# The first pass of a macaron block: when projection weights, tokens and normalisation scales are loaded

## Chip, cores and metric

One core of a Trainium2 chip runs the whole program in one launch. The metric is the device time in microseconds (us), as the median of several runs; a profile of one more execution says where the time goes. The core's engines are TensorE (PE, matrix products into PSUM), VectorE (DVE), ScalarE (ACT, activations with a scale and a bias), GpSimd (POOL) and SyncE (SP, which here only issues transfers). Each engine executes its own instructions in the order in which the program lists them, and semaphores order the engines among each other.

## The reference

The input is 4 x 1024 tokens of 1024 float32 values. Every block works on normalised tokens and adds its result to the tokens:

```python
x = x + 0.5 * ffn(layernorm(x), weight, bias, centroids, assignments)
x = x + attn(layernorm(x), Wq, bq, Wk, bk, Wv, bv)
x = x + 0.5 * ffn(layernorm(x), weight, bias, centroids, assignments)

def ffn(x, ...):                       # 1024 -> 1024, gated
    dots = softmax(x @ centroids.T / 0.1, axis=-1)     # 64 clusters
    hits = dots > 0.01
    query_sel, cluster_sel = any(hits, axis=1), any(hits, axis=0)
    row_sel = cluster_sel[assignments]
    dense = x @ weight.T + bias
    return where(query_sel[:, None] & row_sel[None, :], dense, 0)

def attn(x, ...):                      # per token, over the 32 x 32 head dimension
    q, k, v = projections of x with 32, 8 and 8 heads; k, v repeated 4 times
    scores = einsum('bsdh,bseh->bsde', q, k) / sqrt(32)
    return einsum('bsde,bseh->bsdh', softmax(scores), v)
```

Because `cluster_sel` is taken over all tokens, no row of the first FFN can be masked before the logits of all tokens are known. This divides the kernel into three passes over the tokens.

## The kernel before

The 4096 tokens are `NT` = 32 tiles of 128 tokens. In the first pass the FFN product of every tile is made and stored (`d1`); the second adds it masked, makes the attention and the logits of the second FFN; the third makes the second FFN's product and the output. The change lies in the first pass alone.

The first pass has steps t = 0 to 31. Two tiles a, a+1 are multiplied together in `winograd`: seven block products of four 128-deep blocks each (tile `st`, L284), in place of eight. A pair takes two steps: the odd step t (a = t - 3) issues four of the products, the next even step the other three. Additions of the products into the result `d` (L275) are DVE's work, straight out of PSUM, and some products accumulate onto a bank that an addition has read before. The last 256 columns and the 64 logits of a tile are made apart: in steps up to 7 and from 28 on by `logits` (tile `ff`, L212), one per step; for the tiles 8 to 27 (`GATED`) by `last_two` (tile `la`, L348), which runs beside `winograd` in the same steps. Steps 8, 9 and 10 hold neither: they have only the three, four and three products of the pairs (4, 5) and (6, 7).

PE needs a tile transposed (`xT`). Tiles 0 to 4 are normalised and transposed on PE. From tile 5 (`BLOCKED`) on it goes another way, over several steps:

- `load_x` (L152) loads the tile token by row, as `x`, only for its moments: `moments` takes two `bn_stats` (L162) on DVE and a root on ACT (L165), `scales` a reciprocal (L171) and a product (L173) on DVE. `block_scales` stores the two numbers of each token in DRAM as `scd`, with a transfer issued by ACT (L648).
- `spread` (L497) loads them as `scb`, so that each partition has the scales of four tokens; it takes four transfers, one for each strip of 32 partitions.
- `load_blocks` (L490) loads the tile a second time as `xb`, in blocks of 32 tokens by 32 columns, with four transfers.
- `from_blocks` normalises the four parts of `xb` on ACT (L505, four activations) and transposes the blocks on DVE (L509).
- `token_sums` makes the four sums that `winograd` needs of a pair, on POOL (L257 to L260), in the odd steps.

What is done in which step is written out by hand. Step t first issues on SP the loads of x(t+5) and xb(t+4) (`loads`), then `spread(t+3)`, and in odd steps two stores of `d1`. `block_scales(t+4)`, the step's logits, the first product with its addition, and `from_blocks(t+1)` follow. At the end of the step the generator `weights` issues a transfer of the projections' weights, which the second pass needs, and one step later does the work on it: `wq` (tile `qn`, L582, 512 KB) in steps 3 to 10 with a reduction on DVE (L586, 1.21 us), `wk` and `wv` (tile `kv`, L597, 128 KB each) in steps 11 to 18 with two copies on POOL (L602), then four blocks of the FFN's weights from SBUF to DRAM (`wtd`, L628). `x`, `xb`, `xT`, `d`, `qn`, `kv` and the token sums all take their place from one pool of `ROWS` = 26 rows of 4 KB per partition; a new row may wait for the last user of the old one.

Of the kernel before, what the change touches and what calls it, by code (L numbers as in the profile page):

```python
# [15 lines left out]
P = 128  # L16
# [26 lines left out]
def kernel(  # L43
# [97 lines left out]
    def strip(i):  # L141
        return slice(i * QROW, (i + 1) * QROW)

    def rows(ap, t):
        return ap[t * P : (t + 1) * P, :]

    def row(name):
        return data.tile([P, EMB], F32, tag="row", bufs=ROWS, name=name)
# [321 lines left out]
    with (  # L470
# [21 lines left out]
        def spread(flat, t):  # L492

            sb = small.tile([P, 4, 2], F32, tag="scb", bufs=4, name=f"scb{t}")
            src = flat.rearrange("(i t) e -> t i e", i=4)
            for j in range(4):
                nc.sync.dma_start(out=sb[strip(j)], in_=src)  # L497
            return sb

        def from_blocks(t, sb):  # L500

            b = xb.pop(t)
            for i in range(4):
                bi = b[:, :, i]
                nc.scalar.activation(  # L505
                    bi, bi, AF.Identity, bias=sb[:, i, 1:2], scale=sb[:, i, 0:1]
                )
            t_ = row(f"xT_1_{t}")
            nc.vector.transpose(t_, b.rearrange("p k i c -> p (k i c)"))  # L509
            return t_.rearrange("p (k c) -> p k c", c=P)  # L510
# [61 lines left out]
        columns(6)  # L572
        ahead(1)

        def weights(step):


            if step < KT:

                k = step  # L580
                qn = row(f"qn{k}").rearrange("p (c r) -> p c r", r=REP)
                nc.sync.dma_start(  # L582
                    out=qn, in_=wq[k * P : (k + 1) * P].rearrange("p d (g r) -> p (d g) r", r=REP)
# [5 lines left out]
                    AX.X,  # L589
                    ALU.add,  # L590
                )
            elif step < 2 * KT:
                k = step - KT
                kvs = row(f"kv{k}")
                kv = {i: kvs[:, (i - 1) * D * HKV : i * D * HKV] for i in (1, 2)}
                for i, src in ((1, wk), (2, wv)):
                    nc.sync.dma_start(  # L597
                        out=kv[i], in_=src[k * P : (k + 1) * P].rearrange("p d h -> p (d h)")
                    )
                yield  # L600
                for i in kv:
                    nc.gpsimd.tensor_copy(  # L602
                        by_head(wqkv[:, k, :], i), kv[i].rearrange("p (d h) -> p d h", h=HKV)
                    )
            elif step == NT - 6:
                bn = row("bn_q").rearrange("p (c r) -> p c r", r=REP)
                nc.sync.dma_start(
                    out=bn.rearrange("p c r -> p (c r)"),
                    in_=bq.rearrange("d h -> (d h)").partition_broadcast(P),
                )  # L610
                bss = row("bs")
                bs = {i: bss[:, (i - 1) * D * HKV : i * D * HKV] for i in (1, 2)}
                for i, src in ((1, bk), (2, bv)):
                    nc.sync.dma_start(
                        out=bs[i], in_=src.rearrange("d h -> (d h)").partition_broadcast(P)
                    )
                yield
                nc.vector.tensor_reduce(
                    by_head(bqkv, 0), bn.rearrange("p (d g) r -> p d g r", g=HKV), AX.X, ALU.add
                )  # L620
                for i in bs:
                    nc.gpsimd.tensor_copy(
                        by_head(bqkv, i), bs[i].rearrange("p (d h) -> p d h", h=HKV)
                    )
            elif step < 2 * KT + 5:

                i = step - 2 * KT - 1
                nc.sync.dma_start(out=wtd[i], in_=blocks(wc)[i])  # L628
            elif step == 2 * KT + 6:
                next(qsums)  # L630
            elif step == NT - 7:
                asg = load_assigned()
                yield
                hot.append(one_hot(asg))

        pending = iter(())
        sc, sb, ss, es, ge = {}, {}, {}, {}, {}
# [4 lines left out]
        qts = w12, w11, w21, w22  # L642
        qsums = weight_sums(blocks(wqkv), qts, [nc.gpsimd] * 4)

        def block_scales(t):
            sc[t] = dram.tile([P, 2], F32, tag="scd", bufs=5, name=f"scd{t}")
            own = scales(moments(xt.pop(t), f"1_{t}"), f"1_{t}")
            nc.scalar.dma_start(out=sc[t], in_=own)  # L648

        def loads(t):  # L650
            if t + 5 < NT:
                load_x(t + 5, rows(xf, t + 5), 1)
            if BLOCKED <= t + 4 < NT:
                load_blocks(t + 4)

        def logits(t):
            dt_[t] = row(f"d1_{t}")
# [3 lines left out]
        for t in range(3):  # L661
# [13 lines left out]
            if t + 2 < BLOCKED:  # L675
                ahead(t + 2)
            for i in (5, 6) if t == 2 else ():
                block_scales(i)

        for t in range(3, NT):  # L680

# [4 lines left out]
            if t % 2 == 1 and t > 4:  # L686
                for i in (a, a + 1):
                    nc.sync.dma_start(out=d1[i], in_=dt_.pop(i))
            if t + 4 < NT:
                block_scales(t + 4)  # L690
            if t not in GATED:
                es[t] = logits(t)
            if t == 3:
# [8 lines left out]
                    steps = zip(steps, last_two(a, a + 1, s4, te, ge))  # L702
            if t < NT - 1:
                next(steps)
            if t > 3:
                i = t + 1
                if i in sb:
                    xT[i] = from_blocks(i, sb.pop(i))
            for i in sorted(es):
                if i >= t - 3 and not isinstance(es[i], tuple):  # L710
                    es[i] = gate_exp(es[i], i, 0)
# [14 lines left out]
                ss[t - 1] = token_sums(xT, t - 1, t, 1)  # L726
            for _ in pending:
                pass
            pending = weights(t - 3)
            next(pending, None)  # L730


# [484 lines left out]
```

## Time and profile before

| | us |
|---|---|
| median of 3 runs | 1323.7 (1322.91 to 1324.2) |
| the profiled execution | 1323.88 |
| its span, first to last instruction | 1322.2 |
| TensorE busy in it | 1301.0 (98%) |
| VectorE, GpSimd, ScalarE busy | 871.0, 583.3, 495.1 |
| mean granted TensorE clock | 0.997 of full speed |

The page also says that the span moved 214.25 MB at a mean of 162 GB/s. In the lines further down, a row of a timeline gives start and duration in us, then engine, line, operation and the tiles written and read; in brackets stands the idle time before it and what ended that. In the chain of waits (the work that ended last, followed back from the end) a row gives start, duration and what it was. A row of the waits gives who waited for what, the total in us, the number of waits and the longest. "SPq" is SP's queue. Matmuls overlap a little, so that eight of 128x384 show 2.74 us in the timeline and 2.58 in the chain.

### The profile page before, as it was taken

How to read it: one execution, taken by the hardware profiler on the slowest of the kernel's cores; microseconds unless marked ns; L12 is line 12 of the kernel's file. 1: busy time of each engine (PE TensorE's matmuls, PEld its weight loads, DVE VectorE, ACT ScalarE, POOL GpSimd, SP SyncE). 2: the span in 40 equal slices, each digit the busy share in tenths (PEclk: the TensorE clock that was granted, in tenths of full speed). 3: DMA queues.
4: the chain of work that ended last, by engine and by line, in shares of the span. 5: the costliest groups of instructions: out<-in, count | busy, mean ns of one | idle time of the engine just before them, and what ended most of it. 6: DMA issues, size and time to landing. Idle time of an engine off the chain costs nothing.

```text
span 1322.2 us, 22786 instructions
## 1 busy us (share of the span) xinstructions
PE 1301.0 (98%) x8726; PEld 840.5 (64%) x8726; DVE 871.0 (66%) x1789; ACT 495.1 (37%) x821; POOL 583.3 (44%) x448
## 2 busy tenths in 40 slices
PE   8998999999999999999999999999999999999998
PEld 7664677777776665666666666666666655555554
DVE  4655555555546358888888888778867448555556
ACT  4432223333210445666666666666643200000000
POOL 3621132232112147566666666666532326634440
PEclk9999899999999999999999999999999999999999
DMA  8487876778614155456666665665551346655532
GB/s 297 86 161 146 170 146 139 167 180 173 124 64 191 43 166 160 153 191 189 195 200 195 189 198 166 200 200 189 163 156 26 104 139 227 239 200 176 178 114 80
DMA packets 296301, 214.25 MB, mean 162 GB/s; under 512 B 240064, under 2 KB 255168, under 8 KB 296192
## 3 DMA queue, kind: packets, MB, share of 16 engines
q1 hardware_dynamic: 278240, 164.78, 46.5%
q0 software_dynamic: 8736, 30.68, 6.3%
q10 hardware_dynamic: 9216, 17.33, 3.6%
q8 instruction: 69, 1.13, 0.4%
q14 instruction: 40, 0.33, 0.1%
HBM read 127.77 MB, written 84.96 MB: 161 GB/s over the span
## 4 chain that ended last, share of the span: by engine, by line
PE 93%; DMA 2%; DVE 2%; ACT 1%; issue 1%; POOL 0%; SPq 0%; ACTq 0%; POOLq 0%; DVEq 0%
PE st L284 40%; PE qs L801 18%; PE ff L212 16%; PE la L348 6%; PE tp L205 4%; PE pq L212 4%; PE sc L877 2%; PE po L919 2%; DMA x<-in_L_attn_x_dram 1%; DVE bn L162 1%; DMA scd<-sc 1%; PE tpw L558 0%; DMA qkvd<-qkv 0%; DMA xb<-in_L_attn_x_dram 0%; DVE d L275 0%
## 5 line engine op out<-in xcount | busy, mean ns | idle before, releaser
L212 PE MATMUL ff<-wc,xT 128*128 128x320 f32 (+1 forms) x768 | 218.1, 438 | 1.7 <-ACT wc L563 0.7
L212 PEld LDWEIGHTS ff<-wc,xT 128*128 128x128 f32 x768 | 143.7, 190 | 64.1 <-ACT xT L206 1.0
L257 POOL TENSOR_TENSOR ts<-xT 128x512 f32<-128x512 f32 x31 | 41.4, 1335 | 309.6 <-DVE xT L509 172.7
L284 PE MATMUL st<-wc,xT 128*128 128x384 f32 x496 | 170.5, 487 | 0.0
L275 DVE TENSOR_TENSOR d<-st,d 128x384 f32<-128x384 f32 x157 | 86.1, 550 | 109.8 <-PE st L284 108.5
L284 PE MATMUL st<-ws,ts 128*128 128x384 f32 x384 | 131.2, 486 | 0.9 <-DVE d L275 0.9
L857 POOL TENSOR_TENSOR kd<-qk,tmask 128x1024 f32<-128x1024 f32 x32 | 60.6, 1893 | 161.9 <-DMA qk<-qkvd 144.5
L284 PEld LDWEIGHTS st<-wc,xT 128*128 128x128 f32 x496 | 93.3, 191 | 60.4 <-issue 1.3
L284 PE MATMUL st<-wqkv,ts 128*128 128x384 f32 x360 | 121.3, 486 | 0.0
L162 DVE BATCH_NORM_STATS2 bn<-x 128x6 f32<-128x512 f32 x132 | 84.3, 680 | 40.4 <-DMA x<-in_L_attn_x_dram 38.2
L801 PE MATMUL qs<-wc,ts_2q 128*128 128x384 f32 x312 | 106.2, 490 | 0.0
L452 DVE SCALAR_TENSOR_TENSOR d<-d,qsel,mask 128x1024 f32<-128x1024 f32 (+2 forms) x68 | 102.8, 1512 | 0.1
L463 POOL TENSOR_TENSOR x<-x,d 128x1024 f32<-128x1024 f32 x32 | 75.5, 2358 | 59.5 <-DVE d L452 46.6
L165 ACT ACTIVATE mv<-mv,eps 128x1 f32<-128x1 f32 x66 | 19.4, 295 | 219.6 <-DVE mv L164 213.1
L284 PEld LDWEIGHTS st<-ws,ts 128*128 128x128 f32 x384 | 71.1, 190 | 44.2 <-issue 2.2
L284 PEld LDWEIGHTS st<-wqkv,ts 128*128 128x128 f32 x360 | 68.3, 190 | 48.1 <-issue 0.8
L275 DVE TENSOR_TENSOR d<-st,brow 128x384 f32<-128x384 f32 x93 | 51.3, 551 | 56.6 <-PE st L284 56.5
L284 PE MATMUL st<-wc,ts 128*128 128x384 f32 x248 | 85.1, 486 | 0.0
L206 ACT COPY xT<-tp 128x512 f32<-128x512 f32 x138 | 73.1, 581 | 30.8 <-PE tp L205 29.9
L801 PEld LDWEIGHTS qs<-wc,ts_2q 128*128 128x128 f32 x312 | 58.2, 190 | 40.5 <-issue 2.6
L948 POOL TENSOR_TENSOR x<-x,ot 128x1024 f32<-128x1024 f32 x32 | 78.1, 2442 | 2.5
L205 PE MATMUL tp<-ident,xn 128*128 128x128 f32 x552 | 73.0, 275 | 3.2 <-ACT xn L180 1.7
(143 smaller groups left out, 2248.2 us busy)
## 6 DMA issues: line engine op xcount, KB each, us to landing
x<-in_L_attn_x_dram SPq DMA_DIRECT2D x64, 512.0 KB, 4.6
d<-d SPq DMA_DIRECT2D x64, 512.0 KB, 4.8
out_dram<-x ACTq DMA_DIRECT2D x30, 512.0 KB, 4.7
xb<-in_L_attn_x_dram SPq DMA_DIRECT2D x108, 128.0 KB, 5.0
y<-x POOLq DMA_DIRECT2D x26, 512.0 KB, 3.1
xTd<-xT POOLq DMA_DIRECT2D x26, 512.0 KB, 5.7
xT<-xTd SPq DMA_DIRECT2D x26, 512.0 KB, 4.9
x<-y SPq DMA_DIRECT2D x26, 512.0 KB, 5.1
```

What stands on the lines that cost most here:

```text
L162: nc.vector.bn_stats(st[:, i, :], src[:, i * 512 : (i + 1) * 512])
L205: nc.tensor.transpose(tp[:, j, :], xn[:, k * P : (k + 1) * P], ident)
L206: nc.scalar.copy(t_[:, 4 * h : 4 * h + 4, :], tp)
L212: nc.tensor.matmul(p, src[:, k, :], wts[:, k, lo:hi], start=(k == 0), stop=(k == KT - 1))
L275: nc.vector.tensor_tensor(out, ps, other, ALU.add)
L284: nc.tensor.matmul(ps, src[:, k, :], wts[:, k, :], start=(k == 0 and onto is None), stop=(k == 3), skip_group_check=onto is not None,)
L348: nc.tensor.matmul(ps, src[:, k, :], wts[:, k, :], start=(k == 0 and onto is None), stop=(k == 3), skip_group_check=onto is not None,)
L452: nc.vector.scalar_tensor_tensor(d[:, sl], d[:, sl], qsel[which][:, t : t + 1], mask[:, sl], ALU.mult, ALU.mult)
L463: nc.gpsimd.tensor_tensor(xt[t], xt[t], dt_.pop(t), ALU.add)
L801: nc.tensor.matmul(ps, src[:, k, :], wts[:, k, :], start=(k == 0 and onto is None), stop=(k == 3), skip_group_check=onto is not None,)
L857: nc.gpsimd.tensor_tensor(kd, qk[:, :, D:].unsqueeze(2).to_broadcast([P, NBLK, 4, D]), tmask.unsqueeze(1).unsqueeze(3).to_broadcast([P, NB ...
L948: nc.gpsimd.tensor_tensor(xv, xv, ov, ALU.add)
```

## The change

Four things are changed, all in the first pass. (1) `weights` takes the step t itself: `wq` is loaded in steps 3 to 5 and 11 to 15, `wk` and `wv` two blocks at a time in steps 16 to 19, the FFN's blocks in steps 20 to 23; steps 6 to 10 load no weights. (2) From step 7 on the loads of `x` move one step ahead (step 7 loads x12 and x13, a later step t loads x(t+6)), and those of `xb` one step back (x(t+3); none in step 7). (3) `scd` is stored in the order in which the partitions need it, 32 rows of eight numbers, and `spread` is one transfer that reads these rows four times. (4) The four activations of `from_blocks(t+1)` become `blocks_normed`, issued on ACT ahead of the root of tile t+4; `block_scales` is split, and its reciprocal, product and store come behind the transposition.

```diff
--- before.py
+++ after.py
@@ -492,19 +492,20 @@
         def spread(flat, t):
 
             sb = small.tile([P, 4, 2], F32, tag="scb", bufs=4, name=f"scb{t}")
-            src = flat.rearrange("(i t) e -> t i e", i=4)
-            for j in range(4):
-                nc.sync.dma_start(out=sb[strip(j)], in_=src)
+            src = flat.unsqueeze(0).to_broadcast([4, QROW, 8])
+            nc.sync.dma_start(out=sb.rearrange("p i e -> p (i e)"), in_=src)
             return sb
 
-        def from_blocks(t, sb):
-
-            b = xb.pop(t)
+        def blocks_normed(t, sb):
             for i in range(4):
-                bi = b[:, :, i]
+                bi = xb[t][:, :, i]
                 nc.scalar.activation(
                     bi, bi, AF.Identity, bias=sb[:, i, 1:2], scale=sb[:, i, 0:1]
                 )
+
+        def from_blocks(t):
+
+            b = xb.pop(t)
             t_ = row(f"xT_1_{t}")
             nc.vector.transpose(t_, b.rearrange("p k i c -> p (k i c)"))
             return t_.rearrange("p (k c) -> p k c", c=P)
@@ -572,12 +573,12 @@
         columns(6)
         ahead(1)
 
-        def weights(step):
-
-
-            if step < KT:
-
-                k = step
+        def weights(t):
+
+
+            if 3 <= t < 6 or 11 <= t < 16:
+
+                k = t - 3 if t < 6 else t - 8
                 qn = row(f"qn{k}").rearrange("p (c r) -> p c r", r=REP)
                 nc.sync.dma_start(
                     out=qn, in_=wq[k * P : (k + 1) * P].rearrange("p d (g r) -> p (d g) r", r=REP)
@@ -589,20 +590,31 @@
                     AX.X,
                     ALU.add,
                 )
-            elif step < 2 * KT:
-                k = step - KT
-                kvs = row(f"kv{k}")
-                kv = {i: kvs[:, (i - 1) * D * HKV : i * D * HKV] for i in (1, 2)}
-                for i, src in ((1, wk), (2, wv)):
+            elif 16 <= t < 20:
+                k = 2 * (t - 16)
+                kvs = row(f"kv{k}").rearrange("p (k w c) -> p k w c", k=2, w=2)
+                for i, src in ((0, wk), (1, wv)):
                     nc.sync.dma_start(
-                        out=kv[i], in_=src[k * P : (k + 1) * P].rearrange("p d h -> p (d h)")
+                        out=kvs[:, :, i],
+                        in_=src[k * P : (k + 2) * P].rearrange("(k p) d h -> p k (d h)", k=2),
                     )
                 yield
-                for i in kv:
-                    nc.gpsimd.tensor_copy(
-                        by_head(wqkv[:, k, :], i), kv[i].rearrange("p (d h) -> p d h", h=HKV)
-                    )
-            elif step == NT - 6:
+                for j in range(2):
+                    for i in range(2):
+                        nc.gpsimd.tensor_copy(
+                            by_head(wqkv[:, k + j, :], i + 1),
+                            kvs[:, j, i].rearrange("p (d h) -> p d h", h=HKV),
+                        )
+            elif 20 <= t < 24:
+
+                nc.sync.dma_start(out=wtd[t - 20], in_=blocks(wc)[t - 20])
+            elif t == 25:
+                next(qsums)
+            elif t == NT - 4:
+                asg = load_assigned()
+                yield
+                hot.append(one_hot(asg))
+            elif t == NT - 3:
                 bn = row("bn_q").rearrange("p (c r) -> p c r", r=REP)
                 nc.sync.dma_start(
                     out=bn.rearrange("p c r -> p (c r)"),
@@ -622,16 +634,6 @@
                     nc.gpsimd.tensor_copy(
                         by_head(bqkv, i), bs[i].rearrange("p (d h) -> p d h", h=HKV)
                     )
-            elif step < 2 * KT + 5:
-
-                i = step - 2 * KT - 1
-                nc.sync.dma_start(out=wtd[i], in_=blocks(wc)[i])
-            elif step == 2 * KT + 6:
-                next(qsums)
-            elif step == NT - 7:
-                asg = load_assigned()
-                yield
-                hot.append(one_hot(asg))
 
         pending = iter(())
         sc, sb, ss, es, ge = {}, {}, {}, {}, {}
@@ -642,16 +644,19 @@
         qts = w12, w11, w21, w22
         qsums = weight_sums(blocks(wqkv), qts, [nc.gpsimd] * 4)
 
-        def block_scales(t):
-            sc[t] = dram.tile([P, 2], F32, tag="scd", bufs=5, name=f"scd{t}")
-            own = scales(moments(xt.pop(t), f"1_{t}"), f"1_{t}")
-            nc.scalar.dma_start(out=sc[t], in_=own)
+        def block_scales(t, mv):
+            sc[t] = dram.tile([QROW, 8], F32, tag="scd", bufs=5, name=f"scd{t}")
+            own = scales(mv, f"1_{t}")
+            nc.scalar.dma_start(out=sc[t].rearrange("t (i e) -> i t e", i=4), in_=own)
 
         def loads(t):
-            if t + 5 < NT:
-                load_x(t + 5, rows(xf, t + 5), 1)
-            if BLOCKED <= t + 4 < NT:
-                load_blocks(t + 4)
+
+            for i in (t + 5,) if t < 7 else (t + 5, t + 6) if t == 7 else (t + 6,):
+                if i < NT:
+                    load_x(i, rows(xf, i), 1)
+            i = t + 4 if t < 7 else t + 3
+            if BLOCKED <= i < NT and t != 7:
+                load_blocks(i)
 
         def logits(t):
             dt_[t] = row(f"d1_{t}")
@@ -675,7 +680,7 @@
             if t + 2 < BLOCKED:
                 ahead(t + 2)
             for i in (5, 6) if t == 2 else ():
-                block_scales(i)
+                block_scales(i, moments(xt.pop(i), f"1_{i}"))
 
         for t in range(3, NT):
 
@@ -686,8 +691,11 @@
             if t % 2 == 1 and t > 4:
                 for i in (a, a + 1):
                     nc.sync.dma_start(out=d1[i], in_=dt_.pop(i))
+            ahead_b = t + 1 in sb and t > 3
+            if ahead_b:
+                blocks_normed(t + 1, sb.pop(t + 1))
             if t + 4 < NT:
-                block_scales(t + 4)
+                mv = moments(xt.pop(t + 4), f"1_{t + 4}")
             if t not in GATED:
                 es[t] = logits(t)
             if t == 3:
@@ -702,10 +710,10 @@
                     steps = zip(steps, last_two(a, a + 1, s4, te, ge))
             if t < NT - 1:
                 next(steps)
-            if t > 3:
-                i = t + 1
-                if i in sb:
-                    xT[i] = from_blocks(i, sb.pop(i))
+            if ahead_b:
+                xT[t + 1] = from_blocks(t + 1)
+            if t + 4 < NT:
+                block_scales(t + 4, mv)
             for i in sorted(es):
                 if i >= t - 3 and not isinstance(es[i], tuple):
                     es[i] = gate_exp(es[i], i, 0)
@@ -726,7 +734,7 @@
                 ss[t - 1] = token_sums(xT, t - 1, t, 1)
             for _ in pending:
                 pass
-            pending = weights(t - 3)
+            pending = weights(t)
             next(pending, None)
 
 
```

## Prediction, made before the changed kernel ran

> **What bounds the kernel now.** I read the page first. It says that TensorE (PE) is busy for 98% of the span, so only its idle or slow time can be won.
>
> ```profile
> PE 1301.0 (98%) x8726; PEld 840.5 (64%) x8726; DVE 871.0 (66%) x1789; ACT 495.1 (37%) x821; POOL 583.3 (44%) x448
> ...
> PEclk9999899999999999999999999999999999999999
> ```
>
> One slice of the clock row is an 8: near 132 to 165 us, in the first pass. PE's waits in that pass (30 to 420 us) hold one large entry:
>
> ```profile
> PE st L284 <- DVE d L275: 7.2, 3, 4.0
> ```
>
> Three stalls, 7.2 us, each for a VectorE (DVE) add out of PSUM. The table of windows, cut at the chain's first product of each step, places them (time; busy time of PE, PEld, DVE, ACT, POOL; clock; DMA share; GB/s):
>
> ```profile
> 88.39:103.03 14.64, 14.64 (x50) 9.13 (x49) 8.04 (x17) 5.28 (x9) 4.75 (x4) 1.00 0.66 153
> 103.03:113.18 10.15, 7.83 (x24) 4.31 (x24) 6.16 (x15) 3.65 (x6) 0.00 (x0) 1.00 0.71 194
> 113.18:124.50 11.32, 10.46 (x33) 6.00 (x32) 5.43 (x11) 2.37 (x5) 4.98 (x4) 1.00 0.86 125
> 124.50:139.21 14.71, 10.71 (x26) 5.71 (x25) 7.99 (x14) 2.37 (x5) 1.68 (x2) 0.79 0.78 143
> ...
> 164.90:190.60 25.70, 25.70 (x115) 18.28 (x114) 13.98 (x42) 7.44 (x14) 7.28 (x8) 1.00 0.73 147
> ```
>
> Rows two to four are steps 8, 9 and 10. They are the short ones: their logits come later with `last_two`, so they hold only three, four and three products. Step 7 before them and the pair 11/12 type after them (fifth row) keep PE full. PE's timeline shows the idle times and the slow stretch:
>
> ```profile
> 110.50 2.85 PE L284 MATMUL st<-ws,xT 128*128 128x384 f32 x8 [2.32 <-DVE d L275]
> ...
> 121.94 5.40 PE L284 MATMUL st<-ws,ts 128*128 128x384 f32 x16 [0.86 <-DVE d L275]
> ...
> 133.92 5.49 PE L284 MATMUL st<-ws,xT 128*128 128x384 f32 x8 [4.00 <-DVE d L275]
> ```
>
> The last product took 5.49 us where its like take 2.74; the windows view gives 134 to 140 us a clock of 0.52. Why is the add late? DVE works in order, and the chain of waits from 110 us on shows what stands in front of it:
>
> ```profile
> 110.01 3.76 DMA scd<-sc
> ...
> 113.84 5.11 DMA x<-in_L_attn_x_dram
> ...
> 118.97 1.30 DVE bn L162 x2
> ...
> 121.37 4.44 DMA scd<-sc
> ...
> 125.88 0.35 SPq L152
> ```
>
> A ring: tokens `x` land, `bn_stats` runs, ACT takes the root, `scd` goes out, and SP's next `x` load (L152) is released only when it lands; the add of the next step stands behind the `bn_stats` of that load. SP's waits confirm it:
>
> ```profile
> SPq L152 <- DMA scd<-sc: 41.7, 11, 6.4
> ```
>
> One round is 125.88 - 113.84 = 12.0 us. A paired step of 12.85 us (25.70/2) covers that; steps of 7.7 and 10.3 us do not.
>
> **The change part by part.** *What can be won.* A product is 2.58 us (chain, x8), so steps 8 to 10 need 10 x 2.58 = 25.8 us. They took 10.15 + 11.32 + 14.71 = 36.2. The excess is 10.4: idle 2.32 + 0.86 + 4.00 = 7.2, and slow matmuls (5.49 - 2.74) + (3.05 - 2.74, the next product) = 3.1, the rest rounding. Between 30 us and the pass's end the waits list no other PE stall over 0.4, so 10.4 us is also the ceiling.
>
> *Tokens sooner.* From step 8 `x(t+6)` is loaded in place of `x(t+5)`, after a double load in step 7; `bn_stats` of x(t+4) thus has two steps of lead, 18 us over a short pair, against a landing of 5.1. That cuts the ring: SP may still wait for `scd` before an `x` load, but nothing in that step reads the load. No bytes are added; rows rise by one for a step and blocks give one back (`xb(t+3)`). An extra wait for a free row: SP's row waits today are 0.2 to 0.6 each, I take 0, at most 1.7 (the longest PE-released one).
>
> *Weights out.* Five `qn` loads (0.33 to 0.79 us of SP each, 512 KB) and five 1.21 us reductions on DVE leave steps 6 to 10 and their successors. In steps 8 to 10 DVE sheds one reduction a step, each in front of that step's `bn_stats`. They go to steps 11 to 15, where DVE is busy 13.98 of 25.70 us: two more per pair make 16.4. `kv` becomes 8 loads of 256 KB, not 16 of 128, in steps 16 to 19: SP issue falls by some 8 x 0.4 us; POOL's 0.63 us copies become four a step, 2.5 us, behind the token sums and with 7.3 of 25.7 busy. Bytes per step there go from 256 to 512 KB: at the 190 GB/s of the busiest rows +1.4 us per 12.85, a DMA share from 0.73 to about 0.84. PE cost 0, covered by the two-step lead; without it, a late `x` would hold DVE as it does today, about 2.3 to 4 us a time. One `wtd` copy (five issues today, four then, 768 KB) goes too.
>
> *Scales by one transfer.* Four `scb` issues take 2.1 to 2.3 us of SP a step; one takes 0.5. I save 1.7 us of SP a step (27 times), none of it on PE's path. Rows and rules part here. The Trainium skill (DMA: Bandwidth & Descriptors, "Rules for kernel authors") says that transfers under 64 KB are mostly overhead and should be merged; at its fixed 2 us three fewer would be 6 us a step. The row says that the four overlap: 2.5 us to landing. I go by the row. The same page ("Why a DMA increments its semaphore by 16 and not by 1") speaks against the change: a transfer uses as many engines as divide the slowest dimension of both sides, at most 16. `[4, 32, 8]` would leave `scb` on 4 engines, and the write in the order `i t e` likewise `scd`. No row has such a transfer. Nearest: in 38 to 60 us the ACT queue's 576 packets took 1.6% of 16 engines, 5.6/576 = 10 ns each; 32 per engine in place of 8 is +0.2 us. Bounds: 0.1 less if the engine count does not matter, and some 4 us more each, from the 2.5 and 4.1 medians to the slowest landings (4.8, 6.6) and as much again for queueing. I take +0.2. Cover: scales written in step t are used in t+3, at least 18 us away, so the sum is the same by row or rule.
>
> *Blocks ahead of the root.* Today in step 8 DVE waits 1.70 us for the root behind a table load, then transposes late (idle 2.13 for ACT's four 0.52 us normalisations). With these first on ACT and reciprocal and scale behind the transposition, that 1.70 + 0.37 leaves the front of the add. Added: the scales go out about 3 us later; ACT's root, exponentials and `scd` now queue behind normalisations that wait for `xb` and `scb`. Those were issued two steps earlier (longest `xb` landing 10.8), so I take 0; a gain is excluded after step 10, as PE has no stall there; the loss is priced as the third rival.
>
> *Check of step 8.* DVE leaves step 7 at 105.2; without reduction and root wait `bn_stats` ends by 106.8 and the add by 107.4. PE reaches the dependent product at 108.2: no stall. Steps 9 and 10 have tokens landed long before. What is late next is DMA: steps 6 to 10 carry 6 `x`, 4 `xb`, 4 `d1`, 14 x 512 KB; at 190 GB/s 38.6 us, in 52.5 us of PE work. It fits.
>
> *Sum.* Profiled execution 1323.9 (span 1322.2 and 1.7 around it) less 10.4 = **1313.5**. It stands 0.2 above the median of the runs, 1323.7, less than their spread.
>
> **The rivals.** *Part of the stall stays.* Steps 3 to 6 keep the lead of one, and x12 and x13 share step 7 with stores; if they come late by a `scd` that is now 3 us later, the first two stalls stay (3.2 us) and the third goes with its slow clock: 1323.9 - 7.1 = 1316.8. For it: SP ran behind before step 8 too (its `x` issue at 88.84). Against: `x` for step 8 went out at 96.13 and was not waited for. The rule weighs here: the rows give a full clock after 2.32 us idle and 0.52 after 4.00; the skill (TensorE: Matmul & The Clock Gate, Part 1) sets the drop at about 3.4 us of idling. By it a remaining stall of 3 us costs 3; by the row of 4.00 it would cost 6, and the time would be 1319.9.
>
> *It does not do what it says.* If the ring closes elsewhere (normalisation waits for `scb`, which waits for `scd`, now behind the transposition), the round stays near 12 us and so does the time: 1323.9. Against: with scales three steps ahead no such round is one step long.
>
> *Slower: `xb` at the head of ACT.* It is now loaded a step later and in steps 11 to 23 stands beside 512 to 768 KB of weights per step. If it lands late, ACT stops, the transposition and all adds behind it on DVE are late, and PE stalls in each step. Price: in the step at 164.90 the transposition ended at 177.0 and DVE then idled 1.25 us for PE; the adds that free the next product's bank had some 2 more. From a slip of about 3.3 us every further us is PE's. At 1.2 us lost in 13 steps: 1313.5 + 15.6 = 1329. It decides from 0.8 a step. Against: `xb` must land more than 25 us after issue, and the longest takes 10.8.
>
> **How the numbers follow.** Full removal 0.67 (1312.3 to 1315); part 0.16 (1315 to 1320.5); no effect 0.08 (1321 to 1326); slower 0.09 (1327 to 1335). About 0.2% (2.6 us) is what a measurement of this kernel can tell from no change. The range 1312.3 to 1320.5 holds 0.83. Faster is the first two and a little of the third, 0.84; same 0.07; slower 0.09.
>
> **What would show it.** Right: `st` <- `d` gone from PE's waits or under 1 us; steps 8 to 10 in 26 us; no clock below 0.99 there; `pq` starting near 433.5 and not 443.87; 27 `scb` issues; `bn` waits for `x` well below 38.2 us. Wrong: idle PE at new places after 130 us (third rival), the 12 us round still in the chain (second), or a stall of 2 to 3 us in steps 7 to 9 (first).

## The result, and the profile after

| | before | after |
|---|---|---|
| median of 5 runs, same chip | 1324.2 us (1322.91 to 1329.0) | 1313.72 us (1312.16 to 1318.14) |
| ratio, 95% interval | 1 | 0.9917 [0.9901, 0.9933] |
| profiled execution, span | 1323.88, 1322.2 us | 1314.23, 1312.4 us |
| mean granted clock | 0.997 | 0.999 |

The changed kernel is faster by 0.83%, some 10.5 us at the medians. The page of the profile after, first and second part:

```profile
PE 1299.8 (99%) x8726; PEld 841.5 (64%) x8726; DVE 878.2 (67%) x1789; ACT 493.8 (38%) x821; POOL 580.7 (44%) x448
...
PEclk9999999999999999999999999999999999999999
```

PE works as long as before within 1.2 us, in a span that is 9.8 us shorter, and the 8 in the clock's row is gone. All of PE's waits from 30 to 420 us (who for what, total us, times, longest):

```profile
PE ff L212 <- ACT xT L206: 0.6, 2, 0.3
PE bT L431 <- DVE best L414: 0.4, 1, 0.4
```

No product `st` waits for an addition `d` any more; before it was 7.2 us in three stalls. The windows by step (start:end; PE, PEld, DVE, ACT, POOL; clock, DMA share, GB/s): step 7, then 8, 9, 10, then the first product of step 11, and a later stretch as long as a pair of steps:

```profile
90.03:104.66 14.63, 14.63 (x49) 9.12 (x49) 7.64 (x17) 6.26 (x12) 3.24 (x3) 1.00 0.56 144
104.66:112.40 7.74, 7.74 (x25) 4.56 (x25) 5.99 (x15) 2.73 (x5) 2.30 (x2) 1.00 0.52 103
112.40:122.72 10.32, 10.32 (x33) 6.08 (x33) 4.48 (x9) 3.29 (x7) 2.69 (x3) 1.00 0.61 180
122.72:130.46 7.74, 7.74 (x25) 4.56 (x25) 5.37 (x11) 2.33 (x5) 2.86 (x3) 1.00 0.68 133
130.46:133.04 2.58, 2.58 (x10) 1.52 (x10) 1.96 (x4) 0.34 (x2) 2.14 (x2) 1.00 0.34 61
165.00:190.70 25.70, 25.70 (x114) 18.28 (x113) 16.46 (x44) 7.78 (x16) 5.04 (x4) 1.00 0.73 166
```

PE's busy time equals the length of every row. Steps 8 to 10 take 25.80 us where they took 36.2, and the clock is 1.00 in each. The last row, from step 13 into step 15, shows what the moved weights cost: DVE is busy for 16.46 us in the length of a pair, where the pair 13/14 had 13.98 before, and PE is busy throughout. (The pair 13/14 itself, now at 156.16 to 181.86, has 16.49 us of DVE and a DMA share of 0.79, 0.73 before.) The chain of waits says the same in three pieces:

```profile
90.03 4.31 PE ff L212 x16
94.34 38.70 PE st L284 x120
133.04 1.09 PE la L348 x8
```

Fifteen products without a gap (38.70/2.58), up to the first `la` (L348). Before, that product started at 142.26.

**DVE in step 8**, from its timeline (start, duration, line, operation), shows in which order the work stood before:

```profile
105.22 1.22 DVE L586 TENSOR_REDUCE wqkv<-qn 128x256 f32<-128x1024 f32 x1
106.35 1.28 DVE L162 BATCH_NORM_STATS2 bn<-x 128x6 f32<-128x512 f32 x2
109.57 0.16 DVE L171 RECIPROCAL sc<-mv 128x1 f32<-128x1 f32 x1 [1.70 <-ACT mv L165]
109.90 0.55 DVE L275 TENSOR_TENSOR d<-st,d 128x384 f32<-128x384 f32 x1
```

and in which order it stands now:

```profile
106.85 1.28 DVE L162 BATCH_NORM_STATS2 bn<-x 128x6 f32<-128x512 f32 x2
108.17 0.21 DVE L164 BATCH_NORM_AGGREGATE mv<-bn 128x2 f32<-128x12 f32 x1
108.29 0.50 DVE L275 TENSOR_TENSOR d<-st,d 128x384 f32<-128x384 f32 x1
108.71 1.23 DVE L510 STREAM_TRANSPOSE xT<-xb 128x1024 f32<-128x1024 f32 x1
110.08 0.16 DVE L171 RECIPROCAL sc<-mv 128x1 f32<-128x1 f32 x1
```

No reduction stands ahead of the `bn_stats`, no root ahead of the addition, and the reciprocal comes behind the transposition. In the pass DVE's waits for the root fall from 25.9 to 1.6 us, and `bn_stats` waits no longer for `x` there (33.5 us before). SP, however, still waits for stored scales (its waits, 30 to 420 us):

```profile
SPq L490 <- DMA scd<-sc: 65.9, 10, 13.3
...
SPq L152 <- DMA scd<-sc: 39.5, 6, 7.2
SPq L496 <- DMA scd<-sc: 34.7, 9, 7.5
```

The longest is 13.3 us; at L152 before it was 6.4. PE does not notice. The experiments begin at these waits, for `load_x` (L152) and `load_blocks` (L490) read nothing of `scd`.

### The profile page after: what moved, and what is told of

Same layout as the page of the kernel before. It is cut to its first block, busy times and chain, and to the rows that moved or that the text cites. A ratio compares the mean times of both kernels' runs of the same rounds, so it can differ in the third digit from the quotient of the medians.

```text
span 1312.4 us, 22675 instructions
## 1 busy us (share of the span) xinstructions
PE 1299.8 (99%) x8726; PEld 841.5 (64%) x8726; DVE 878.2 (67%) x1789; ACT 493.8 (38%) x821; POOL 580.7 (44%) x448
## 4 chain that ended last, share of the span: by engine, by line
PE 96%; DVE 2%; ACT 1%; DMA 1%; issue 0%; ACTq 0%
PE st L284 42%; PE qs L809 18%; PE ff L212 16%; PE la L348 6%; PE tp L205 4%; PE pq L212 4%; PE sc L885 2%; PE po L927 2%; PE tpw L559 1%; DVE bn L162 0%; DMA x<-in_L_attn_x_dram 0%; DVE d L452 0%; PE pm L446 0%; ACT xT L206 0%; ACT L190 0%
## 5 line engine op out<-in xcount | busy, mean ns | idle before, releaser
L452 DVE SCALAR_TENSOR_TENSOR d<-d,qsel,mask 128x1024 f32<-128x1024 f32 (+2 forms) x68 | 106.4, 1565 | 0.2
```

Source lines behind the costliest of these rows:

```text
L452: nc.vector.scalar_tensor_tensor(d[:, sl], d[:, sl], qsel[which][:, t : t + 1], mask[:, sl], ALU.mult, ALU.mult)
```

## The experiments

Every kernel was timed in three rounds beside the kernel before on the same chip. To see where a gain comes from I read one number from the chain of each profiled execution (in before_shift, whose chain runs elsewhere, from PE's timeline): the time from the end of step 7's work to the first `la`, which is 28.38 us in the kernel after (eleven products of 2.58). What a kernel takes beyond that is its *excess*; the kernel before has 39.23 - 28.38 = 10.85. "Stalls" is the row PE `st` <- DVE `d` of the waits from 30 to 420 us (total, times, longest). Both belong to one execution, and the medians to several: the profiled execution of only_tok took 5.3 us more than its median, that of only_wts 4.6 us more, that of the kernel before 0.3 to 3.1 us less than its medians in this table.

| kernel | median, us | before, us | ratio [95%] | stalls, us | excess, us |
|---|---|---|---|---|---|
| after | 1313.72 | 1324.2 | 0.9917 [0.9901, 0.9933] | none | 0 |
| only_tok | 1319.3 | 1326.53 | 0.9954 [0.9936, 0.9971] | 2.7, 2, 2.3 | 4.9 |
| only_wts | 1318.67 | 1326.53 | 0.9945 [0.9928, 0.9961] | 3.1, 3, 1.2 | 1.7 |
| only_spr | 1318.05 | 1326.53 | 0.9937 [0.9918, 0.9956] | 2.7, 2, 2.3 | 3.25 |
| only_blk | 1314.16 | 1326.53 | 0.9908 [0.9891, 0.9925] | 0.2, 1, 0.2 | 0.4 |
| before_shift | 1327.14 | 1326.07 | 1.0011 [0.9997, 1.0026] | 5.8, 4, 2.3 | 6.7 |
| wts_keep | 1321.67 | 1326.07 | 0.9962 [0.9948, 0.9976] | 6.5, 3, 3.6 | 8.9 |
| spr_keep | 1338.53 | 1326.07 | 1.0095 [1.0062, 1.0129] | 15.9, 9, 5.8 | 14.0 |
| no_blk | 1315.44 | 1326.07 | 0.9934 [0.9912, 0.9955] | 1.2, 1, 1.2 | 1.4 |
| swap | 1328.61 | 1326.38 | 1.0016 [1.0007, 1.0026] | 8.2, 3, 5.4 | 13.3 |
| tok_keep | 1320.32 | 1326.38 | 0.9953 [0.9936, 0.997] | 2.7, 2, 2.3 | 4.9 |
| no_tok | 1314.05 | 1326.38 | 0.9906 [0.9886, 0.9925] | none | 0 |
| swap_late | 1322.1 | 1326.98 | 0.9966 [0.9954, 0.9977] | 4.6, 2, 2.3 | 6.8 |

The theory at the start was the prediction's, called A: the lead of the tokens cuts the ring, and without it the ring stays. Its rivals were that the weights do it by their bytes and their reductions (B), that DVE's order does it, with the wait for the root (C), or that each part does a share. The first four runs made a further theory necessary, D, which is told behind them.

### Each part alone

**only_tok**: the kernel before with the loads of the change.

```diff
-            if t + 5 < NT:
-                load_x(t + 5, rows(xf, t + 5), 1)
-            if BLOCKED <= t + 4 < NT:
-                load_blocks(t + 4)
+            for i in (t + 5,) if t < 7 else (t + 5, t + 6) if t == 7 else (t + 6,):
+                if i < NT:
+                    load_x(i, rows(xf, i), 1)
+            i = t + 4 if t < 7 else t + 3
+            if BLOCKED <= i < NT and t != 7:
+                load_blocks(i)
```

> Of the change, the tokens alone: x(t+6) from step 8 on, two in step 7, xb(t+3). Theory A (the ring x, bn_stats, root, scd, x sets the round of 12 us, and the lead cuts it): the second and third stall go with the slow clock (0.9 + 4.0 + 3.1 us), the first stays in part, since the reduction of 1.21 us and the wait of 1.70 us for the root still stand in front of the add in step 8; about 1315 to 1317 us. Theory B (the weights' 512 KB and 1.21 us per step are what makes the tokens late): at most 2 us are gained, 1322 or more.

**only_wts**: the kernel before with the weights in the change's steps.

```diff
-            if step < KT:
+            if 3 <= t < 6 or 11 <= t < 16:
...
-            pending = weights(t - 3)
+            pending = weights(t)
```

> Of the change, the weights' loads alone out of steps 6 to 10. Theory A: the ring still has to be walked once per step, x lands perhaps 1 us sooner; steps 8 to 10 still take near 12 us each, 1 to 3 us gained, 1321 to 1323. Theory B: the steps are freed and nearly all comes back, 1314 to 1316.

**only_spr**: the kernel before with `scd` in the new order and one transfer in `spread`.

```diff
-            for j in range(4):
-                nc.sync.dma_start(out=sb[strip(j)], in_=src)
+            src = flat.unsqueeze(0).to_broadcast([4, QROW, 8])
+            nc.sync.dma_start(out=sb.rearrange("p i e -> p (i e)"), in_=src)
...
-            nc.scalar.dma_start(out=sc[t], in_=own)
+            nc.scalar.dma_start(out=sc[t].rearrange("t (i e) -> i t e", i=4), in_=own)
```

> Of the change, the scales' layout alone: scd stored in the order of the partitions, scb by one transfer. Both theories: no gain, since SP waits for scd, not for its own issue time: 1323 to 1325. If the 4-row outer dimension keeps the transfers on fewer engines, scd lands later and the ring of theory A grows by as much in each of steps 8 to 10: up to 3 us slower.

**only_blk**: the kernel before with the activations ahead of the root, and reciprocal, product and store behind the transposition.

```diff
+            if ahead_b:
+                blocks_normed(t + 1, sb.pop(t + 1))
             if t + 4 < NT:
-                block_scales(t + 4)
+                mv = moments(xt.pop(t + 4), f"1_{t + 4}")
...
+            if t + 4 < NT:
+                block_scales(t + 4, mv)
```

> Of the change, the order alone: normalisation of the blocks ahead of the root, reciprocal, product and store behind the transposition. Theory A: the first stall (2.3 us) shrinks as the 1.70 us wait for the root leaves the front of the add, but scd goes out 2 to 3 us later, so that the ring's round grows from 12 to 14 or 15 us and the second and third stall grow: 1324 to 1329, no gain and rather slower. Theory C (DVE's order, the wait for the root, is the cause): the stalls go, 1314 to 1317.

All four are faster than before, by 0.46, 0.55, 0.63 and 0.92%. Added up that is 2.56%, three times what the four give together, so they are not shares of a sum: they remove the same thing. And the fourth alone gives the whole. Its chain of waits, in which only the first addition of step 8 still stands ahead of PE:

```profile
110.15 23.49 PE st L284 x72
133.64 1.09 PE la L348 x8
```

Nine products follow without a gap, though `x` has its old lead of one step. Theory A falls: the lead is not needed. (only_tok has stalls of 2.31 and 0.41 us and no longer those of 0.86 and 4.00; that the lead is enough for this is shown only by tok_keep, further down, since only_tok changes the order of the transfers as well.) only_tok and only_wts took times between what A and B forecast for them. C met its forecast for only_blk, and is put to the test with no_blk. The transfer that I had priced at nothing on PE's path, only_spr, is worth 8 us by itself, which no theory had forecast.

What ties an `x` load to a store of scales that it does not read? I read it from the program as built. Each transfer that SP or ACT issues takes the next of eight semaphores in turn, and it is issued only when the transfer eight places before it has landed. The numbers are fixed when the program is built, in one order for both engines. The order in the kernel before around step 8 (number of the semaphore, and whose landing it waits for):

```
ACT scd12  5
SP  scb10  6   scb9
SP  scb10  7   qn3
SP  scb10  0   x12
SP  scb10  1   xb11
SP  d1_2   2   xb11
SP  d1_3   3   xb11
SP  qn4    4   xb11
SP  x13    5   scd12      <- eighth behind scd12
```

The next one is the same: x14 is eighth behind scd13. So the edge that closes the ring is one of counting (theory D): `scd` must land before whichever transfer is the eighth behind it. Anything that changes the number or the order of transfers moves the edge. The waits of SP name the new eighth. In only_spr, with three transfers fewer a step, it is mostly a part of `xb`:

```profile
SPq L490 <- DMA scd<-sc: 119.4, 19, 12.1
```

The total is almost three times that of L152 before, and harmless, since `xb` stands behind the step's `x` in SP's queue and is used three steps later. In only_blk, where `scd` is stored later in the step, the edge falls on the stores of `d1` and on weights:

```profile
SPq L690 <- DMA scd<-sc: 18.7, 8, 4.2
```

SP's timeline shows what this does to `x` (x13, then a `qn` load, then x14):

```profile
104.48 1.15 SPq L152 DMA_DIRECT2D x<-in_L_attn_x_dram  x1
115.30 0.35 SPq L584 DMA_DIRECT2D qn<-in_L_attn_Wq_dram  x1
115.76 0.37 SPq L152 DMA_DIRECT2D x<-in_L_attn_x_dram  x1
```

x13 no longer waits; before, it went out at 113.84. The `qn` load is the eighth behind scd12, and x14 stands behind it in the queue, so x14 is still held. But its `bn_stats` comes at 126.01, a step later than that of x13: one round of the ring now has two steps of time.

### Does the count alone do it?

If D holds, added transfers should move the edge without any of the four parts. **before_shift** puts one transfer of 1 KB, which nothing reads, behind each of the eight `qn` loads.

```diff
+        def tiny(name):
+            dm = small.tile([P, 2], F32, tag="dm", name=f"dm_{name}")
+            nc.sync.dma_start(out=dm, in_=wk[:P, 0, 0:2])
...
                 )
+                tiny(step)
```

> The kernel before, and behind each of its eight qn loads one more transfer of 1 KB that nothing reads. Nothing is taken away. Theory D (the ring is closed by the count of transfers: each takes one of eight semaphores in turn and waits for the one eight before it, and in steps 8 and 9 that makes the x load wait for the scales just written): the x load is now the ninth behind scd, waits for a block load instead, and the second and third stall go; 7 to 9 us below the kernel before, with one stall of some 2.3 us left in step 8. Theory A and B (the tokens' real dependences, or the load of work in the short steps): the same time as the kernel before, or some tenths slower.

It gained nothing that can be measured, 1.0011 [0.9997, 1.0026]. Its chain shows why (L577 is the added transfer):

```profile
111.78 3.23 DMA scd<-sc
115.03 0.33 SPq L577
...
115.46 4.38 DMA x<-in_L_attn_x_dram
```

The eighth is now the added transfer, but it stands directly ahead of the `x` load in SP's queue, which executes in order. The edge moved by one place and the ring went on. D had forecast a gain of 7 to 9 us and missed, for it counted places and left out that a held transfer also holds what stands behind it in the queue. With this added the run fits D; it does not prove it.

The opposite test keeps a part and puts the count back. **wts_keep** is only_wts with a transfer of 1 KB in place of each of the five moved `qn` loads. The 512 KB and the reductions stay away; only the number of transfers is that of before.

```diff
+            elif 6 <= t < 11:
+                tiny(t)
```

> The weights alone out of steps 6 to 10 as in only_wts, with a transfer of 1 KB that nothing reads in place of each of the five, so that the count of transfers and with it what x waits for is that of the kernel before. Theory D: the ring stays, and at most 3 us of the gain are left (each round a little shorter by the 1.21 us reduction and the 512 KB). Theory B: as only_wts, 7 us below the kernel before.

```profile
108.97 5.97 DMA scd<-sc
114.96 3.76 DMA x<-in_L_attn_x_dram
...
121.14 4.88 DMA scd<-sc
...
126.08 4.33 DMA x<-in_L_attn_x_dram
```

The ring is back with a round of 126.08 - 114.96 = 11.1 us, 0.9 shorter than before, and so are 6.5 us of stalls, where only_wts has one of 1.19 us in these steps (its other two, 0.96 and 0.91, come at 221 and 325 us). Moving 512 KB and a reduction out of each step did not cut the ring; moving a *transfer* did. By its excess the kernel should gain 1.9 us. At the medians it gained 4.4, between the forecasts of D (at most 3) and B (7), so that the time alone does not decide and the chain does. The two profiled executions differ by 1323.88 - 1321.76 = 2.1 us, as the excess says; the rest lies in the spread of the kernel before, whose median here is 2.2 us above its profiled execution.

**spr_keep** is only_spr with three such transfers behind each `spread`.

```diff
             nc.sync.dma_start(out=sb.rearrange("p i e -> p (i e)"), in_=src)
+            for j in range(3):
+                dm = small.tile([P, 2], F32, tag="dm", name=f"dm_{t}_{j}")
+                nc.sync.dma_start(out=dm, in_=wk[:P, 0, 0:2])
```

> The scales by one transfer as in only_spr, with three transfers of 1 KB that nothing reads behind it, so that the count is again that of the kernel before. Theory D: the ring and the three stalls are back, within 2 us of the kernel before. If the single transfer itself is what gained: as only_spr, 8 us below.

It is slower than before, 1.0095 [1.0062, 1.0129], with nine stalls. Back in the count of before, the gain of 8 us is gone. But it is worse than the kernel before by 12 us, where D forecast at most 2, so it is no clean return to it. Three of the stalls (9.5 us) lie in steps 8 to 10; the other six (6.4 us) come after 180 us, where the kernel before has none. In its chain `scd` takes 7.64 and 4.92 us to land (3.76 and 4.44 before), and the added transfers' tiles (`dm`) bring waits of their own (SP waits for `dm` 26 times, 39.0 us in all). Whether the new order of `scd` makes its store slower by itself is not told apart here.

### The order alone

**swap** changes nothing but the order: in steps 7 to 11 the `x` load that the next step would issue first goes directly ahead of the `qn` load, at the end of the step.

```diff
-            if t + 5 < NT:
+            if t + 5 < NT and (t < 8 or t > 12):
                 load_x(t + 5, rows(xf, t + 5), 1)
...
+            if 7 <= t < 12:
+                load_x(t + 6, rows(xf, t + 6), 1)
             pending = weights(t - 3)
```

> The kernel before with two transfers exchanged in SP's queue at the end of steps 7 to 11: the next step's x load goes ahead of the qn load in place of behind it. Nothing is added or taken away. Theory D as it now stands (SP issues in order, and the transfer eight behind scd waits for scd to land; the ring closes when that is x itself or one ahead of x): qn becomes the eighth and waits in place of x, x goes out at once; the second and third stall go with the slow clock and the first of 2.3 us stays: 6 to 9 us below the kernel before, as only_wts, only_spr and only_tok. If what gained there was work or bytes taken out: within 2 us of the kernel before.

Measured 1.0016 [1.0007, 1.0026]: no gain, where D led me to expect 6 to 9 us. The `x` load is indeed no longer held. The chain shows what is:

```profile
112.09 4.90 DMA scd<-sc
...
117.05 4.16 DMA qn<-in_L_attn_Wq_dram
...
121.23 1.22 DVE wqkv L586
122.45 1.20 DVE bn L162 x2
...
124.75 4.99 DMA scd<-sc
...
129.82 4.85 DMA qn<-in_L_attn_Wq_dram
```

The `qn` load is now the eighth. Its reduction (L586) stands ahead of `bn_stats` on DVE, so the ring closes through the weights: `scd`, `qn`, reduction, `bn_stats`, root, `scd`, a round of 129.82 - 117.05 = 12.8 us. Five pairs of transfers exchanged their places, and the ring took another body of the same length.

**swap_late** takes that body away: swap, with the reductions of `qn` one step later in steps 8 to 12. It issues the same transfers in the same order as swap.

```diff
-            for _ in pending:
-                pass
+            while len(pend) > (1 if 8 <= t < 13 else 0):
+                for _ in pend.pop(0):
+                    pass
...
-            pending = weights(t - 3)
-            next(pending, None)
+            pend.append(weights(t - 3))
+            next(pend[-1], None)
```

> As swap (x ahead of qn at the ends of steps 7 to 11, so that qn is the eighth transfer behind scd and waits for it), and in addition the reduction of qn on DVE is made one step later for the loads of these steps. The same transfers and the same work as the kernel before, in another order. In swap the ring went on through qn: scd, qn, its reduction in front of bn_stats, root, scd. Theory D (any transfer that DVE needs ahead of its next bn_stats closes the ring): nothing that waits for scd is now needed in the same step; the second and third stall go and the first of some 2.3 us stays: 6 to 9 us below the kernel before. If it is something else that only_wts, only_spr and only_tok took away (bytes, issue time, the double lead): within 3 us of the kernel before.

0.9966 [0.9954, 0.9977], 4.9 us at the medians and less than the 6 to 9 that I expected: stalls of 2.32 and 2.24 us are left of 8.2. The chain ends the second one thus:

```profile
119.07 6.77 DMA xb<-in_L_attn_x_dram
...
125.91 6.00 DMA x<-in_L_attn_x_dram
```

SP was held at `qn` till 116.61, so `xb` went out late. The next `x` is the eighth behind a part of this `xb`, so it went out only when that had landed, and itself landed at 131.91 for a `bn_stats` in the same step. The ring through `scd` is open, but the queue and the count behind its old place carry the delay for one step.

### Is the lead of any use, and are all four parts needed?

**tok_keep** gives only_tok a transfer of 1 KB at the head of step 9, ahead of `x`. In the program as built this makes that `x` (x15) the eighth behind scd13; in only_tok a part of `xb` is.

```diff
+            if t == 9:
+                dm = small.tile([P, 2], F32, tag="dm", name="dm")
+                nc.sync.dma_start(out=dm, in_=wk[:P, 0, 0:2])
```

> Tokens alone as in only_tok, and one transfer of 1 KB that nothing reads at the head of step 9, so that there SP again waits for scd ahead of the x load, as it did in the kernel before. Theory D with the lead of two steps: SP waits, but the tokens it loads are not read for another step; as only_tok, 6 to 8 us below the kernel before. If the lead protects from nothing: the third stall comes back, 2 us or less below the kernel before.

Same as only_tok, 0.9953 and 0.9954, with the same stalls and excess. The added transfer went out at 118.89 and `x` at 124.09, after 4.7 us of waiting for `scd`, yet PE's waits did not change: with a step of lead this late `x` cost nothing. That much of the prediction's step is shown, for one load.

**no_tok** is the kernel after with the loads of before; **no_blk** is the kernel after with the normalisation and the scales of before.

```diff
# no_tok
-            for i in (t + 5,) if t < 7 else (t + 5, t + 6) if t == 7 else (t + 6,):
-                if i < NT:
-                    load_x(i, rows(xf, i), 1)
+            if t + 5 < NT:
+                load_x(t + 5, rows(xf, t + 5), 1)
...
# no_blk
-            if ahead_b:
-                blocks_normed(t + 1, sb.pop(t + 1))
             if t + 4 < NT:
-                mv = moments(xt.pop(t + 4), f"1_{t + 4}")
+                block_scales(t + 4)
...
```

> The changed kernel with x and xb loaded in the old steps. Theory D: the count of transfers puts a block load, behind x, at the eighth place, the root is out of the way; as the changed kernel, 0 to 1 us above it (0.991 to 0.993 of the kernel before). Theory A of the prediction (the lead is what cuts the ring): at least 5 us above it.

> The changed kernel with the order of blocks and root put back. Theory D: no ring, but the root's 1.70 us are in front of the add again; in step 8 a stall of some 1 to 2 us comes back in part (2.3 before, less the 1.21 us reduction that is gone), so 0 to 2 us above the changed kernel. Theory C (the order carries the gain by itself): 7 to 10 us above it.

no_tok loses nothing: 0.9906 [0.9886, 0.9925], no stall, excess 0. no_blk keeps one stall, PE's timeline showing it in step 8:

```profile
111.16 2.85 PE L284 MATMUL st<-ws,xT 128*128 128x384 f32 x8 [1.19 <-DVE d L275]
```

That is the root and the scales ahead of the addition. It is 2.3 us in kernels that also have the reduction there, 1.19 where the weights were moved, and 0.2 or none with the fourth part. Of the three stalls of before, then, the first is the root's and the reduction's, and the other two are the ring's. Theory C falls here as well: it forecast 7 to 10 us above the kernel after, and no_blk lies 1.7 above it, within D's 0 to 2. Of the versions here only_blk and no_tok (0.9908 and 0.9906) measure level with the kernel after (0.9917). None is better than it clear of the intervals, and PE's remaining stalls in the pass of the kernel after add up to 1.0 us.

Read from the programs as built, the place behind scd12 and scd13 fits the third stall, the one of 4.00 us before. Where the eighth is the `x` of the next tile (the kernel before, wts_keep, spr_keep), a transfer directly ahead of it (before_shift) or the next `qn` load (swap, swap_late), that stall is 2.1 us or more. Where it is a part of `xb`, a part of `scb` or a store, it is 0.4 us or none. only_blk and tok_keep are the two in which the edge still reaches an `x`, but that of the tile after next, and their third stall is 0.4 us or none too.

## Why the prediction was right, and where it was not

**The sum.** 1313.5 was predicted and 1313.72 measured, 1314.23 in the profile. The place and the size hold: steps 8 to 10 in 25.80 us (predicted 25.8), no wait of `st` for `d`, the clock at 1.00. From the end of step 7 to the first `la` the gain is 39.23 - 28.38 = 10.85, against 10.4; the rest lies in the first product of step 11, which was also slow before. The prediction counted 0.31 us of this product into the 10.4 of steps 8 to 10, where it does not belong, so that 0.45 us there, not rounding alone, stay unassigned.

**`pq`** starts at 434.65, predicted 433.5. The profiled execution lost 1.64 us before step 3: its first transposing products on PE, the same code, took nearly twice as long (`tp` x8 1.97 us, 1.09 before). Other kernels of this study start step 3 at 39.4 us or at some 41, so this is the execution and not the change. The attention gave back 0.85 by a shorter wait for its input (1.1 us, 2.0 before), which is no part of the sum either.

**"That cuts the ring".** This is the step that failed, although its number came true. I gave the cut to the tokens' lead. The lead does protect (tok_keep), but no_tok is as fast as the kernel after without it, and only_blk reaches the same with nothing but the fourth part. I had taken SP's wait for `scd` as a fixture of the `x` load. It was a product of counting, and three other parts move it too. The four parts open the ring more than once, so the time came out right whichever of them was credited; for this step it was luck.

**"None of it on PE's path"**, of the scales' one transfer: wrong when it stands alone (0.9937), right only beside the others. The saving in issue time was sized well enough (27 issues of 0.57 us in place of 108 of 0.43). What I did not price was that three transfers fewer a step make another one wait. The +0.2 us for fewer DMA engines stays open: it was not isolated.

**Weights out.** "DVE sheds one reduction a step" is right (the first stall falls from 2.3 to 1.19 us), and DVE's 16.46 us in a pair is the 16.4 predicted. The DMA share in steps 13 and 14 rose from 0.73 to 0.79 and not to 0.84, so I overrated the price. But much of what only_wts gains came from the absent transfers, a term that this step did not have: with the transfers put back (wts_keep) the gain falls from 7.9 to 4.4 us at the medians, and from 9.1 to 1.9 by the excess.

**Blocks ahead of the root.** The 1.70 + 0.37 us at the front of the addition was the right mechanism: root waits 1.6 us after 25.9, and no_blk brings the stall back. Undervalued was the later store of `scd`, which I listed among the costs; in only_blk it goes with the move of the edge off the next `x`. No run has the fourth part with the old edge, so how much of only_blk's gain is the order and how much the count is not told apart.

**The rivals.** No effect and slower did not come about: `xb` at the head of ACT cost nothing that PE shows. The partial rival was not the kernel after but fits its parts, and there its reading of the clock was too kind, as the last section shows.

## What to carry to other kernels

When a trace shows an instruction waiting for a transfer that it does not read, ask what counts it in: here each transfer waited for the one eight places before it, so adding, merging or reordering transfers anywhere in a step moved a wait from one load to another. Before crediting an edit, run it alone and leave it out alone; four edits that each gain, and whose gains add up to three times the whole, are removing one ring. A gain from a shifted count lasts only until the next edit shifts it back, as wts_keep and spr_keep did. What held in tok_keep was a load with a step to spare.

## What the runs showed of the hardware

An idle time of PE of the same length did not always cost the same. The product behind the first stall in only_tok and in only_spr, from PE's timelines:

```profile
113.06 4.54 PE L284 MATMUL st<-ws,xT 128*128 128x384 f32 x8 [2.31 <-DVE d L275]
```

```profile
110.56 2.85 PE L284 MATMUL st<-ws,xT 128*128 128x384 f32 x8 [2.32 <-DVE d L275]
```

Of the eight kernels with a stall of 2.3 us there, one execution each, it took about 4.5 us in six and 2.85 in two; after 1.19 us of idle time it was always 2.85. The granted clock goes with it: from 112 to 119 us it is 0.76 in each of the six, and from 109 to 116 us it is 1.00 in the two. So 2.3 us of idling can cost some 1.7 more. The later stalls of 2.14 us (before_shift) and 2.24 us (swap_late) left it at 1.00. The prediction had weighed the Trainium skill's figure (TensorE: Matmul & The Clock Gate, Part 1, about 3.4 us) for stalls of this kind; these runs lose speed below it, though not each time. The six are also the ones that began the pass at about 41 us and not 39.4, which is observed and not explained.

The transfers in the new shapes cost their issuing engine more: ACT 0.53 us for `scd` (0.33 before), SP 0.57 for `scb` (0.43).
